# Values of two token tiles by one seven-product multiplication, in a float32 attention kernel with a gate

## The chip, the cores and the metric

The kernel runs on one core of a Trainium2 chip. The metric is the device time of one execution in microseconds (us). TensorE (PE) does matrix products, VectorE (DVE), ScalarE (ACT) and GpSimd (POOL) do elementwise work, and SyncE (SP) issues most transfers. PEld is TensorE's loading of the stationary operand.

## The reference

The input x has 8 batches of 1024 tokens with 512 features, all in float32. With `_layernorm` as usual, the reference is, cut to what matters:

```python
xn = _layernorm(x)
def proj(Wm, bm):                      # 16 heads of 32
    y = einsum('bld,ed->ble', xn, Wm) + bm
    return y.reshape(B, L, H, dk).transpose(0, 2, 1, 3)
q, k, v = proj(Wq, bq), proj(Wk, bk), proj(Wv, bv)
scores = einsum('bhid,bhjd->bhij', q, k) / sqrt(dk)
im = arange(L) % 256
scores = where(im[:, None] >= im[None, :], scores, -1e30)
attn = einsum('bhij,bhjd->bhid', softmax(scores), v)
s = einsum('bld,ed->ble', merge_heads(attn), Wo) + bo
w = (weights >= 0) * 2 - 1
g = silu(clip(einsum('bsi,oi->bso', xn, w) * scale + bias, -100, 100))
out = x + s * g
```

A query sees the keys whose place in their window of 256 is not after its own, in every window. The value product, `xn` with `Wv`, is the one that changes: 1024 x 512 by 512 x 512 in each batch.

## The kernel before

**Tiles.** The 1024 tokens of a batch are dealt to eight token tiles of 128, so that most of the masked part falls on whole tiles that are left out. The normed tokens are turned once into `xnT` (features on partitions). The heads are worked in four groups g of four heads, and each (batch b, group g) has nine steps, n = 0 to 8: 36 steps a batch, 288 in all.

**A step.** Three PSUM uses exist. One tile of four banks, `quad`, holds the scores of a step. It is used twice: first as t, the scores of keys by queries less the row maxima (`probs_quad`, L591 the maxima by matmul, L613 the products), from which ACT takes the exponential p (L626); then as s, scores of queries by keys for the *next* group (`maxima_quad`, L524), from which DVE takes the maxima pm (L536, one reduction or two). So t, exponential, s, reduction, next t form a ring through one PSUM tile. Two banks hold `av`, the sums of p times v (`attend_quad`, L639, a step behind t). The last two banks, `bank(...)`, go in turn to everything else: q, k and v products, gates (y), outputs (o), turned maxima (mT, `shift_rows`, L565, copied out by ACT, L571), turned inputs (xnT) and the sums of p (sum).

`add_probs` (L657) adds the p tiles of a group on POOL, in two running totals, so that the softmax's divisor needs one product with ones (`sum_keys`); for step n it is written in the loop after `attend_quad` of step n, that is a step later than its exponential. ACT copies the sum, DVE inverts it in pieces of 128 columns (`invert`, L714) and multiplies (`normalise_heads`, L718).

**Side work.** TensorE has time in a step between t and s, while ACT works, and between s and the next t, while DVE works. Into these gaps goes side work, in an order written out by hand: `STEADY` for batches 1 to 6, `OPENING` for batch 0, `CLOSING` for batch 7, with one string for each g. V4 is the value product of token tile 4, G2 a gate, q20 the queries of group 2 of the first half of the tokens, O4 an output of the batch before, N0 the layernorm of half of the next batch, W and R turns of Wo and a row of constants, H a gate in plain float32; a prime means the next batch, and what stands before a bar may also be taken early, by the group before. `plan` turns the words into `Work` items, with ACT, DVE, POOL and DMA operations linked some blocks ahead or behind. `Beside.fill` takes items until a wanted time (by the planner's own cost per item) is spent: at least about 1.2 us between t and s, and 2.35 or more between s and the next t. An item whose operands are not written yet is waited for in program order, not skipped, except turns.

`product` makes an item list of one 128 x 512 result: four chunks (one for each 128 features), each of four matmuls that use 32 columns of the array side by side with 512 columns streaming. A chunk can be split at column 192, 256 or 320 to fit what is left of a gap. After the fourth chunk `after` empties the bank: for values one ACT copy (L383). `gate_work` splits the operand in two parts of fewer bits (L427, L428) and makes two passes; DVE and POOL close it (L432, L433, L434), and ACT and DVE finish it later (L438, L441). `output_work` fetches the gate and x again (L728, L730), closes on DVE (L736, L737) and POOL (L738) and stores (L739).

**Start and end.** Before the loop the kernel loads and turns the weights and does the first norms and the first products. After it come the last outputs: `last_output` handles the last tile in two halves of 256 columns (L753, L754 on POOL ahead, L763 the products, L771 and L772 on DVE).

Each engine runs its own instructions in program order; a framework places the semaphores and gives out buffers, so an operation waits for the last reader of the buffer that it writes.

Of the kernel before, what the change touches and what calls it, by code (L numbers as in the profile page):

```python
# [16 lines left out]
P = 128  # L17
# [56 lines left out]
def tile_gated_window_attention(  # L74
# [27 lines left out]
    qk = pool("qk", 3)  # L102
    heads = pool("heads", 6)
    probs = pool("probs", 2)
    total = pool("total", 1)
    tmp = pool("tmp", 5)
    parts = pool("parts", 1)
    rows_p = pool("rows", 1)
    small = pool("small", 4)
    spill = pool("spill", 2, space=bass.MemoryType.DRAM)  # L110
    ps_q = pool("ps_q", 1, space=PSUM)
    ps_a = pool("ps_a", 2, space=PSUM)
# [41 lines left out]
    for it in range(4):  # L154
        load_x(0, it, (nc.sync, nc.scalar)[it % 2])
    fetch_weight("wk", wk, chunks(probs, "p", "wk_st"), [nc.sync, nc.scalar])
    bias_r = temp("bias_r")[0 : 3 * NC, 0:P]
# [10 lines left out]
    for name, src in (("fscale", fscale), ("fbias", fbias), ("bo", bo)):  # L168
# [4 lines left out]
        "wo", wo,  # L173
        [heads.tile([P, 1, D], F32, tag="a0", name=f"wo_st_{o}") for o in range(NC)], [nc.sync],
    )
# [65 lines left out]
    def turn_weight(name):  # L241


        def turn(c):
            if c == 0:
                wT[name] = const.tile(
                    [P, NC, D], F32R if name == "fw" else F32, name=f"{name}T"
                )
            dst = wT[name]
# [11 lines left out]
            if name == "fw":  # L261

                sg = temp(f"sign_{c}")
                nc.vector.tensor_scalar(sg, ps, 0.0, 2.0, ALU.is_ge, ALU.mult)
                nc.vector.tensor_scalar(dst[:, c, :], sg, -1.0, None, ALU.add)
            elif name == "wo":

                nc.scalar.mul(dst[:, c, :], ps, 0.5)
                turned.add(("wo", c))
            elif name == "wk":  # L270
                staged["copy", c] = lambda: (
                    nc.vector.tensor_copy(dst[:, c, :], ps) if c > 1
                    else nc.scalar.copy(dst[:, c, :], ps)
                )
            else:
                evacuate(dst[:, c, :], ps)

        return [lambda c=c: turn(c) for c in range(NC)]


# [97 lines left out]

    def values_work(b, it):
        def after(ps):  # L380

            vt[b, it] = vpool.tile([P, D], F32, tag="v", name=f"v_{b}_{it}")
            nc.scalar.copy(vt[b, it], ps)  # L383

        return product(
            f"v_ps_{b}_{it}",
            [(lambda c=c: (xn_cols(b, it)[:, c, :], wT["wv"][:, c, :])) for c in range(NC)],
            0.86,
            after,
            lambda: (b, it) in turned,  # L390
        )

    def heads_work(b, g, half, which):
# [20 lines left out]
        )  # L414

    def gate_work(b, it, plain=False):

# [4 lines left out]

        def split():
            src = xn_cols(b, it)
            for i in range(2):
                part[i] = parts.tile([P, NC, P], F32R, tag=f"x{i}", name=f"x{i}_{b}_{it}", bufs=2)
            nc.scalar.copy(part[0], src)  # L427
            nc.gpsimd.tensor_tensor(part[1], src, part[0].bitcast(F32), ALU.subtract)  # L428
# [21 lines left out]
        def passes(i):  # L450

            if i == 0:
                hold.append(bank(f"y_ps_{b}_{it}"))
            for c in range(NC):
                nc.tensor.matmul(  # L455
                    hold[0], lhsT=part[i][:, c, :], rhs=wT["fw"][:, c, :],
                    start=(i == 0 and c == 0), stop=(i == 1 and c == NC - 1),
                )
            if i:
                after(hold[0])  # L460

# [22 lines left out]
        )  # L484
        split = Work(0, split, ready=lambda: (b, it) in turned)
        return split, [main], squash, finish
# [160 lines left out]

    def add_probs(b, g, n):

# [11 lines left out]
        for f, j, lo, w, at in segments(n)[0]:  # L661
            if n > TOTAL[f]:
                add(f, n, lo, w, at)
        for f in (0, 1):

            if n == TOTAL[f]:
                for early in range(FIRST[f], n):
# [4 lines left out]
    def keep_sum(b, g, f, ps):  # L672

        aT[b, g, f] = heads.tile([P, HALF], F32, tag=f"a{f}", name=f"aT_{b}_{g}_{f}")
        nc.scalar.copy(aT[b, g, f], ps)  # L675
# [49 lines left out]
    def output_work(b, it):  # L725
        def fetch():
            g = xres.tile([P, D], F32, tag="io", name=f"gb_{b}_{it}")
            nc.sync.dma_start(g, gd[b][it])  # L728
            xr = xres.tile([P, D], F32, tag="io", name=f"xb_{b}_{it}")
            nc.sync.dma_start(xr, tokens(x, b, it))  # L730
# [13 lines left out]
        ]  # L744
        return fetch, product(f"o_ps_{b}_{it}", pairs, 0.86, after, lambda: it in back, True)

# [30 lines left out]
    def row_work():  # L777
# [7 lines left out]
        def after(ps):  # L785
            nc.vector.scalar_tensor_tensor(rows["bo"], rows["bo"], 0.5, ps, ALU.mult, ALU.add)

        return spread, product(
            "bo_ps", [(lambda c=c: (wide[0][:, c, :], wT["wo"][:, c, :])) for c in range(NC)], 0.86, after,
            lambda: bool(wide) and all(("wo", c) in turned for c in range(NC)), True,  # L790
        )

# [8 lines left out]
    STEADY = (  # L801
        "V4 G2 V5 q20 | V7 G3 V6 k20 q21 G4 k21",
        "O4 G5 O5 | q30 N0 k30 O6 q31 G6 k31 G7",
        "N1 O7 O0 | O1 k00' V0' q00' O2 O3 q01'",
        "k01' V1' | q11' G0' V2' k10' G1' V3' k11' q10'",
    )
    OPENING = (
        "V2 G0 V3 V4 G1 V5 V7 V6 G2 k20 q21 k21",
        "G3 q20 q30 N0 k30 | G4 q31 G5 k31 G6 V0'",
        "G7 N1 V1' | k00' q00' W0 V2' W1 V3' W2 q01' W3",  # L810
        "k01' G0' | q11' k10' R G1' k11' q10'",
    )
    CLOSING = (
        "V4 V5 | q20 V7 V6 k20 q21 k21",
        "O4 O5 | q30 k30 O6 q31 O7 k31",
# [17 lines left out]

    blocks, links = [], []

    def link(i, fn, tail=False):
        links.append((i, fn, tail))

    def plan(b, g, text):
        for word in text.split():  # L840
# [26 lines left out]
            elif kind == "V":  # L867
                main = values_work(bb, int(number))
            elif kind == "W":
# [7 lines left out]
            else:  # L877
                split, main, squash, finish = gate_work(bb, int(number), kind == "H")
                if split is not None:
                    link(i - 3, split)  # L880
                later = 1 if b in (0, B - 1) else 0
                link(i + 2 + later, squash)
# [30 lines left out]
    class Beside:  # L913
# [36 lines left out]
        def fill(self, want, kept=None, early=False, turns=1):  # L950
# [5 lines left out]
            while self.work:  # L956
# [15 lines left out]
                elif free and kept is not None:  # L972
                    kept.append(w)
                elif free or spent + w.cost <= want + 0.1:
                    if w.edge:
# [14 lines left out]
                if w.opens:  # L990
                    next_open = since < 9
                since += w.cost
                if w.closes:
# [16 lines left out]
    behind = []  # L1010

    sides = {}

# [15 lines left out]

    idle_turns(44)  # L1030
    for fn in turn_weight("wk"):
        fn()
    stats, scale, normalise, turn = norms[0]
    for k in range(4):
        stats[k]()
        if k % 2:
            scale(k - 1, k + 1)
    for k in range(4):
        normalise[k]()
    staged["copy", 0]()  # L1040
    for k in range(4):
        turn[k]()
        idle_turns(4)
        if k == 1:
            staged["copy", 1]()
    staged["copy", 2]()
    staged["copy", 3]()
    ps = ps_a.tile([P, 512], F32, tag="av", name="bias_ps")
    nc.tensor.transpose(ps[:, 0 : 3 * NC], bias_r, ident[0 : 3 * NC, 0 : 3 * NC])
    nc.scalar.copy(bias_c, ps[:, 0 : 3 * NC])  # L1050
    for w in heads_work(0, 0, 0, "k"):
        w.run()
    more_constants()
# [19 lines left out]

    wv_turns, fw_turns = turn_weight("wv"), turn_weight("fw")
    start = heads_work(0, 0, 1, "k")
    start += woven(heads_work(0, 1, 1, "q"), wv_turns[:2])
    start += woven(heads_work(0, 1, 0, "k"), wv_turns[2:])
    start += values_work(0, 0)
    start += woven(heads_work(0, 1, 1, "k"), fw_turns[:2])
    start += woven(heads_work(0, 1, 0, "q"), fw_turns[2:])  # L1080
    start += values_work(0, 1)
    start = Beside(start, [0] * NQ)
# [12 lines left out]
    for s, (b, g, n) in enumerate(steps):  # L1095
# [12 lines left out]
        def fill(want, kept=None, turns=1):  # L1108

            spent = 0.0  # L1110
            for one in line:
                if spent < want - 0.1:
                    spent += one.fill(want - spent, kept, one is not now, turns)
                if one.work:
                    break
# [3 lines left out]
        if s:  # L1119
# [3 lines left out]
            else:  # L1123
                add_probs(*steps[s - 1])
        if add:
# [7 lines left out]
        if first:  # L1133
            shift_rows(*turn)
        want = max(1.2 - mine, 0.0) if nxt else share
        spent = fill(want, kept, 0)
        if nxt and spent < want - 0.5:
            spent += fill(want - spent, kept)
        share -= spent
        if turn and not first:  # L1140
            shift_rows(*turn)
        if nxt is not None:
# [3 lines left out]
            if n == 8:  # L1146
                shift_parts(0)
        if add:
            invert(*add, 1)
# [15 lines left out]
        spent = now.fill(1e9) if n == NQ - 1 else 0.0  # L1165
        if nxt:
            want = max(share, 2.45 if len(S_QUADS[n]) > 1 else 2.35) - spent
            turned_now = now.turn_ahead()
            want -= turned_now
            want -= fill(want, turns=0 if turned_now else 1)  # L1170
            if want > 0.5:

                want -= fill(want, turns=2)
        if n == NQ - 1:

# [14 lines left out]
    order = (4, 5, 6, 7, 0, 1, 2, 3)  # L1190
    units[4][0]()
    for i, it in enumerate(order):
        if i + 1 < NT:
            units[order[i + 1]][0]()
        if i + 1 < NT and order[i + 1] < 4:
# [56 lines left out]
```

## Time and profile before

| what | value |
|---|---|
| time, median of 3 runs | 2229.66 us (2228.48 to 2230.08) |
| the profiled execution: own time, span | 2227.41 us, 2225.6 us |
| granted TensorE clock in it | 0.999 of full speed |
| busy: PE, POOL, DVE, ACT | 98%, 60%, 57%, 39% |
| first t (L591) of the steps | 77.3 us after the start of the span |
| batches 0 to 6, first t to first t of the next | 272.7, 265.7, 268.5, then 269.25 each (mean of four) |
| last matmul ends, last DVE operation ends | 2216.7, 2222.2 us |
| moved by DMA | 93.60 MB, mean 42 GB/s |
| value products v_ps, L357 | 254.7 us of TensorE matmul busy time, 64 results |

Times inside the kernel come from that one execution. "Busy" is the time that an engine's instructions ran; "idle before, releaser" is the time that the engine stood still before an instruction, and what ended it. A matmul in float32 is recorded as two. The chain that ended last is followed back from the last instruction.

### The profile page before, as it was taken

To read this page: it belongs to the slowest core of one execution; us is meant where nothing else is said; L and a number is where in the kernel's file an instruction comes from. 1 tells how busy PE (TensorE), PEld (TensorE's weight loads), DVE (VectorE), ACT (ScalarE), POOL (GpSimd) and SP (SyncE) were. 2 spreads that over 40 slices of the span, in tenths; PEclk is the share of its full clock that TensorE was granted. 3 is DMA by queue.
4 is the path that set the end of the run, shared out by engine and by line. 5 is a ranking of instruction groups with operands and counts; after the bars stand their busy time and mean duration, and the time that the engine had idled before them with its cause. 6 is when DMAs were issued, how large, how long until landed. Compare 5 with 4: busy or idle time off the path is not lost.

```text
span 2225.6 us, 57271 instructions
## 1 busy us (share of the span) xinstructions
PE 2185.2 (98%) x25989; PEld 858.4 (39%) x25989; DVE 1275.8 (57%) x1635; ACT 875.3 (39%) x862; POOL 1325.8 (60%) x1198
## 2 busy tenths in 40 slices
PE   8999999999999999999999999999999999999998
PEld 4334333343333343333333333344333343333333
DVE  4556556665456655566455655565655665555664
ACT  2244434344334443344434444334434344333331
POOL 1356565666566666576556675557666566665562
PEclk9999999999999999999999999999999999999999
DMA  4001000120001200012000120001100111000113
GB/s 166 3 14 35 11 6 33 50 82 25 25 25 39 81 27 25 25 63 68 16 25 25 63 68 16 25 32 62 62 16 30 40 63 62 7 21 25 44 53 124
DMA packets 49676, 93.60 MB, mean 42 GB/s; under 512 B 5388, under 2 KB 5656, under 8 KB 49432
## 3 DMA queue, kind: packets, MB, share of 16 engines
q1 hardware_dynamic: 48728, 88.76, 12.0%
q8 instruction: 203, 3.33, 0.6%
q10 hardware_dynamic: 704, 1.18, 0.2%
q14 instruction: 41, 0.34, 0.0%
HBM read 56.37 MB, written 33.55 MB: 40 GB/s over the span
## 4 chain that ended last, share of the span: by engine, by line
PE 80%; POOL 6%; DVE 5%; ACT 5%; issue 3%; DMA 1%; SPq 0%; POOLq 0%; ACTq 0%; DVEq 0%
PE s L524 11%; PE av L639 10%; PE t L613 10%; PE v_ps L357 9%; PE q_ps L357 9%; PE k_ps L357 9%; PE o_ps L357 8%; POOL p L657 5%; PE y_ps L455 5%; PE t L591 4%; ACT p L626 4%; DVE pm L536 3%; PE sum L680 2%; PE s L512 1%; PE xnT_ps L327 1%
## 5 line engine op out<-in xcount | busy, mean ns | idle before, releaser
L657 POOL TENSOR_TENSOR p<-p,p 128x512 f32<-128x512 f32 x930 | 1097.7, 1212 | 186.7 <-PE av L639 103.7
L536 DVE TENSOR_REDUCE pm<-s 128x4 f32<-128x2048 f32 (+3 forms) x384 | 663.9, 1750 | 599.0 <-PE s L524 596.8
L626 ACT ACTIVATE p<-t 128x2048 f32<-128x2048 f32 x288 | 541.0, 1878 | 855.8 <-PE t L613 799.9
L714 DVE RECIPROCAL aT<-aT 128x128 f32<-128x128 f32 x256 | 230.3, 928 | 217.8 <-ACT aT L675 217.8
L524 PE MATMUL s<-k,q 32*128 32x512 f32 (+3 forms) x3072 | 315.4, 504 | 7.3 <-ACT p L626 6.5
L639 PE MATMUL av<-p,v 128*32 128x512 f32 (+3 forms) x3072 | 307.4, 495 | 1.6 <-DVE aT L718 1.4
L613 PE MATMUL t<-q,k 32*128 32x512 f32 (+3 forms) x3072 | 306.1, 492 | 0.0
L357 PE MATMUL q_ps<-xnT,wqT 128*32 128x512 f32 (+2 forms) x2656 | 254.5, 497 | 2.0 <-ACT xnT L328 1.0
L357 PE MATMUL k_ps<-xnT,wkT 128*32 128x512 f32 (+2 forms) x2792 | 254.5, 481 | 0.3 <-ACT q L400 0.2
L357 PE MATMUL v_ps<-wvT,xnT 128*32 128x512 f32 (+3 forms) x2720 | 254.7, 490 | 0.0
L357 PE MATMUL o_ps<-woT,aT 128*32 128x512 f32 (+2 forms) x2584 | 243.9, 501 | 1.5 <-ACT shift L571 0.8
L738 POOL TENSOR_TENSOR s<-s,xb 128x512 f32<-128x512 f32 x63 | 86.0, 1365 | 240.6 <-DVE s L737 234.4
L434 POOL TENSOR_SCALAR y<-y 128x512 f32<-128x512 f32 x64 | 39.7, 620 | 276.8 <-DVE y L433 266.4
L428 POOL TENSOR_TENSOR x<-xnT,x 128x512 fp32r<-128x512 f32 x58 | 74.0, 1276 | 165.5 <-ACT x L427 163.1
L613 PEld LDWEIGHTS t<-q,k 32*128 32x128 f32 x3072 | 139.1, 185 | 25.8
L357 PEld LDWEIGHTS k_ps<-xnT,wkT 128*32 128x32 f32 x2792 | 82.5, 109 | 167.6 <-issue 140.5
L357 PEld LDWEIGHTS q_ps<-xnT,wqT 128*32 128x32 f32 x2656 | 78.7, 109 | 174.6 <-issue 151.8
L639 PEld LDWEIGHTS av<-p,v 128*32 128x32 f32 x3072 | 70.3, 108 | 195.9 <-issue 163.4
L357 PEld LDWEIGHTS v_ps<-wvT,xnT 128*32 128x32 f32 x2720 | 78.9, 109 | 168.2 <-issue 143.5
L524 PEld LDWEIGHTS s<-k,q 32*128 32x128 f32 x3072 | 117.0, 184 | 59.9 <-ACT p L626 50.0
L455 PE MATMUL y_ps<-fwT,x 128*128 128x512 f32 x464 | 135.4, 418 | 1.7 <-ACT k L400 1.3
L357 PEld LDWEIGHTS o_ps<-woT,aT 128*32 128x32 f32 x2584 | 76.6, 109 | 152.3 <-issue 134.0
(96 smaller groups left out, 1479.8 us busy)
## 6 DMA issues: line engine op xcount, KB each, us to landing
g<-t SPq DMA_DIRECT2D x64, 256.0 KB, 2.1
gb<-g SPq DMA_DIRECT2D x64, 256.0 KB, 2.9
xb<-in_L_attn_x_dram SPq DMA_DIRECT2D x64, 256.0 KB, 3.3
out_dram<-s SPq DMA_DIRECT2D x63, 256.0 KB, 2.5
x<-in_L_attn_x_dram SPq DMA_DIRECT2D x62, 256.0 KB, 3.1
wq_st<-in_L_attn_Wq_dram SPq DMA_DIRECT2D x2, 512.0 KB, 4.8
wv_st<-in_L_attn_Wv_dram SPq DMA_DIRECT2D x2, 512.0 KB
fw_st<-in_L_ffn_weights_dram SPq DMA_DIRECT2D x2, 512.0 KB, 8.8
```

The source lines that it names most:

```text
L357: nc.tensor.matmul(hold[0][cols, lo:hi], lhsT=lhsT[:, cols], rhs=rhs[:, lo:hi], start=(i == 0 and lo == 0), stop=(i == n - 1), skip_group_ ...
L428: nc.gpsimd.tensor_tensor(part[1], src, part[0].bitcast(F32), ALU.subtract)
L455: nc.tensor.matmul(hold[0], lhsT=part[i][:, c, :], rhs=wT["fw"][:, c, :], start=(i == 0 and c == 0), stop=(i == 1 and c == NC - 1),)
L524: nc.tensor.matmul(sc[:, h, at : at + w], lhsT=qt[b, g][head_rows(h), i * P : (i + 1) * P], rhs=kt[b, g][head_rows(h), lo:hi], start=(at = ...
L536: nc.vector.tensor_reduce(pm[:, 0 if lo == 0 else 1, i, :], sc[:, :, at : at + w], AX.X, ALU.max)
L591: nc.tensor.matmul(sc[:, h, at : at + w], lhsT=neg1[r, :], rhs=shift[b, g, f][r, lo : lo + w], start=(k == 0), stop=False, skip_group_chec ...
L613: nc.tensor.matmul(sc[:, h, at : at + w], lhsT=kt[b, g][head_rows(h), j * P : (j + 1) * P], rhs=qt[b, g][head_rows(h), q0 : q0 + w], start ...
L626: nc.scalar.activation(pt[:, :, :width], sc[:, :, :width], AF.Exp, scale=SCALE)
L639: nc.tensor.matmul(av[b, g, f][head_rows(h), lo : lo + w], lhsT=vt[b, j][:, g * P + h * DK : g * P + (h + 1) * DK], rhs=pts[b, g, n][:, h, ...
L657: nc.gpsimd.tensor_tensor(t[:, hs, lo : lo + w], t[:, hs, lo : lo + w], p[:, hs, at : at + w], ALU.add)
L714: nc.vector.reciprocal(r, r)
L738: nc.gpsimd.tensor_tensor(s, s, xr, ALU.add)
```

## The change

**Values in pairs.** Two value products of token tiles i and j are one product of a 256 x 512 by a 512 x 512 matrix. It is cut into 2 x 2 blocks: the features in halves (X1., X2.), the two token tiles (X.1, X.2), the output columns in halves of 256. Winograd's form of Strassen's multiplication makes the four result blocks from seven block products instead of eight. The four sums S1 to S4 of weight blocks are made once (`sum_blocks`, DVE); the four sums T1 to T4 of token blocks are made by POOL for each pair (`prepare`), while the pair before is at work. The class `Pair` has 14 atoms of four matmuls with 256 columns in four phases, each phase in one bank; two products share a bank's halves, the seventh has a bank alone. `close` empties the phases: 0 by two ACT copies and a POOL add, 1 by three DVE adds, 2 by two ACT copies and two POOL adds, 3 by one DVE add. POOL's adds in a gap before s are put after the reduction is issued (`later`, `defer`). Atoms are not split.

**Around it.** The seven blocks need 14 KB a partition. They share one SBUF tile with Wo: both weights are kept in DRAM (`keep_weight`) and loaded back (`load_weight`) by the words Lo and Lv. The orders are rewritten, with other work between the pairs: words V45, V67 and V01', V23' stand for pairs. The adds of p that go into a total that exists already are written a step earlier, after their own step's s; those that need the total of the step stay (`held`). The parts of a gate have one buffer instead of two, with an order kept. `fill` doesn't open another bank when two are closed behind each other beside a reduction (`shut`), and the loop runs a last closing atom ahead of s if it is ready. The heads pool shrinks from 6 buffers to 5 for one tag.

**Start and end.** wk is requested ahead of the x tiles 2 and 3, and the first keys are made in two halves of 256 tokens. The last outputs fetch two tiles ahead instead of one, with x in another pool, in batch 7.

The order of instructions gives 1792 value matmuls of 256 columns, where there were 688 of 512, 312 of 320 and of 192 columns and 48 of 256. DVE gets 132 adds of 128 x 256 more, ACT 128 copies of 256 columns for 64 of 512, POOL 224 operations of 128 x 256 more.

```diff
@@ product of a pair
-    def values_work(b, it):
-        def after(ps):
-            vt[b, it] = vpool.tile([P, D], F32, tag="v", name=f"v_{b}_{it}")
-            nc.scalar.copy(vt[b, it], ps)
...
+    def sum_blocks():
+        for out, a, b, op in (
+            ("S1", "A21", "A22", ALU.add),
+            ("S3", "A11", "A21", ALU.subtract),
+            ("S2", "S1", "A11", ALU.subtract),
+            ("S4", "A12", "S2", ALU.subtract),
+        ):
+            nc.vector.tensor_tensor(wb[out], wb[a], wb[b], op)
+
+    def keep_weight(name):
+        weight_d[name] = kept_w.tile(list(wb["tile"].shape), F32, tag=name, name=f"{name}_d")
+        nc.sync.dma_start(weight_d[name], wb["tile"])
+        wb["name"] = name
+
+    def load_weight(name):
+        shared_tile(name)
+        nc.sync.dma_start(wb["tile"], weight_d[name])
+        wb["name"] = name
...
+    class Pair:
...
+            phases = (
+                (("X11", "A11"), ("T2", "S2")),
+                (("T3", "S3"), ("T1", "S1")),
+                (("T4", "A22"), ("X22", "S4")),
+                (("X21", "A12"),),
+            )
+
+            def matmul(k, part, c):
+                if part == 0 and c == 0:
+                    hold.append(bank(f"{name}_ps_{k}"))
+                lhs, rhs = phases[k][part]
+                for q in range(NH):
+                    cols = head_rows(q)
+                    nc.tensor.matmul(
+                        hold[k][cols, part * 256 : part * 256 + 256],
+                        lhsT=self.t[lhs][:, c, cols], rhs=wb[rhs][:, c, :],
...
+                if part + 1 == len(phases[k]) and c == 1:
+                    close(k, hold[k])
...
+        def prepare(self):
...
+            for out, a, b in (
+                ("T1", "X12", "X11"), ("T2", "X22", "T1"), ("T3", "X22", "X12"), ("T4", "X21", "T2"),
+            ):
+                nc.gpsimd.tensor_tensor(t[out], t[a], t[b], ALU.subtract)
+            self.prepared = True
...
+        def close(k, ps):
+
+            if k == 0:
+                u[0], u[1] = part_sum(name, 0), part_sum(name, 1)
+                nc.scalar.copy(u[0], ps[:, LO])
+                nc.scalar.copy(u[1], ps[:, HI])
+                later(lambda: plus(u[1], u[1], u[0], nc.gpsimd))
+            elif k == 1:
...
+                plus(u[2], ps[:, LO], u[1])
+                plus(vt[b, j][:, HI], ps[:, HI], u[2])
+                plus(u[3], ps[:, HI], u[1])
+            elif k == 2:
+                y21, y12 = vt[b, i][:, HI], vt[b, j][:, LO]
+                nc.scalar.copy(y21, ps[:, LO])
+                nc.scalar.copy(y12, ps[:, HI])
+                later(lambda: plus(y21, y21, u[2], nc.gpsimd))
+                later(lambda: plus(y12, y12, u[3], nc.gpsimd))
+            else:
+                plus(vt[b, i][:, LO], ps[:, LO], u[0])
@@ adds of p
         for f, j, lo, w, at in segments(n)[0]:
-            if n > TOTAL[f]:
+            if n > TOTAL[f] and not held:
                 add(f, n, lo, w, at)
         for f in (0, 1):
-
-            if n == TOTAL[f]:
+            if n == TOTAL[f] and held:
...
@@ orders
     STEADY = (
-        "V4 G2 V5 q20 | V7 G3 V6 k20 q21 G4 k21",
-        "O4 G5 O5 | q30 N0 k30 O6 q31 G6 k31 G7",
-        "N1 O7 O0 | O1 k00' V0' q00' O2 O3 q01'",
-        "k01' V1' | q11' G0' V2' k10' G1' V3' k11' q10'",
+        "V45 G2 | q20 V67 Lo G3 k20 q21 G4 k21",
+        "O4 O5 G5 O6 O7 | q30 N0 k30 q31 G6 k31 N1 G7",
+        "O0 O1 O2 O3 Lv | k00' q00' k01' q01'",
+        "V01' G0' | q11' V23' k10' G1' k11' q10'",
     )
     OPENING = (
-        "V2 G0 V3 V4 G1 V5 V7 V6 G2 k20 q21 k21",
-        "G3 q20 q30 N0 k30 | G4 q31 G5 k31 G6 V0'",
-        "G7 N1 V1' | k00' q00' W0 V2' W1 V3' W2 q01' W3",
-        "k01' G0' | q11' k10' R G1' k11' q10'",
+        "V23 G0 V45 | G1 V67 k20 G2 q21 k21",
+        "G3 W0 q20 W1 G4 | q30 W2 N0 k30 W3 G5 R q31 Lv N1 G6 k31",
+        "G7 V01' | k00' q00' k01' q01'",
+        "G0' V23' | q11' k10' G1' k11' q10'",
     )
     CLOSING = (
-        "V4 V5 | q20 V7 V6 k20 q21 k21",
+        "V45 | q20 V67 Lo k20 q21 k21",
...
-                later = 1 if b in (0, B - 1) else 0
+                later = 1 if b == 0 else 0
@@ step loop
             else:
-                add_probs(*steps[s - 1])
+                add_probs(*steps[s - 1], held=True)
...
+        defer[0] = kept
         spent = fill(want, kept, 0)
...
+        if nxt:
+
+            ahead = next((w for w in now.work if w.cost), None)
+            if ahead and ahead.closes and ahead.slow and ahead.cost < 0.5 and ahead.ready():
+                spent += fill(ahead.cost, kept, 0)
+        defer[0] = None
...
+        if not last:
+
+            add_probs(b, g, n)
         if add:
             invert(*add, 1)
@@ tail
-    units[4][0]()
+    for it in order[:2]:
+        units[it][0]()
     for i, it in enumerate(order):
-        if i + 1 < NT:
-            units[order[i + 1]][0]()
+        if i + 2 < NT:
+            units[order[i + 2]][0]()
```

## The prediction

> **What bounds the kernel now.** The page comes first: the share of each engine, then the chain that ended last, then the costliest groups.
>
> ```profile
> span 2225.6 us, 57271 instructions
> ...
> PE 2185.2 (98%) x25989; PEld 858.4 (39%) x25989; DVE 1275.8 (57%) x1635; ACT 875.3 (39%) x862; POOL 1325.8 (60%) x1198
> ...
> PE 80%; POOL 6%; DVE 5%; ACT 5%; issue 3%; DMA 1%; SPq 0%; POOLq 0%; ACTq 0%; DVEq 0%
> ...
> L657 POOL TENSOR_TENSOR p<-p,p 128x512 f32<-128x512 f32 x930 | 1097.7, 1212 | 186.7 <-PE av L639 103.7
> L536 DVE TENSOR_REDUCE pm<-s 128x4 f32<-128x2048 f32 (+3 forms) x384 | 663.9, 1750 | 599.0 <-PE s L524 596.8
> L626 ACT ACTIVATE p<-t 128x2048 f32<-128x2048 f32 x288 | 541.0, 1878 | 855.8 <-PE t L613 799.9
> ...
> L357 PE MATMUL v_ps<-wvT,xnT 128*32 128x512 f32 (+3 forms) x2720 | 254.7, 490 | 0.0
> ```
>
> TensorE is busy 98% of the span and carries 80% of the chain. So matmul time is worth what it costs, wherever something else does not set the pace. What that something is shows in one step, from one t to the next, in the timeline of batch 3:
>
> ```profile
> 884.12 0.40 PE L591 MATMUL t<-shift,neg 3*128 3x512 bf16 x4
> ...
> 885.52 1.88 ACT L626 ACTIVATE p<-t 128x2048 f32<-128x2048 f32 x1 [1.43 <-PE t L613]
> ...
> 887.05 0.41 PE L565 MATMUL mT_ps<-identb,mt 128*32 128x128 bf16 x16
> ...
> 887.45 1.14 PE L524 MATMUL s<-k,q 32*128 32x512 f32 x8
> 887.50 0.59 ACT L571 CAST shift<-mT_ps 128x512 bf16<-128x512 f32 x1
> ...
> 888.52 1.92 PE L357 MATMUL v_ps<-wvT,xnT 128*32 128x512 f32 x16
> 888.66 2.29 DVE L536 TENSOR_REDUCE pm<-s 128x4 f32<-128x2048 f32 x1 [0.91 <-PE s L524]
> ...
> 891.50 0.40 PE L591 MATMUL t<-shift,neg 3*128 3x512 bf16 x4
> ```
>
> t and s share the one quad. The exponential ends at 887.40 and s starts at 887.45. The reduction ends at 890.95, and only then may the next t start; here it starts 0.55 later, since values and gate matmuls fill TensorE to 891.50. A step has thus a floor: s no earlier than 3.35 after t, the next t no earlier than 3.55 after s, 6.9 in all (up to 7.35 for n = 5, 6, 8, which have a second reduction). Side work up to the floor is free; above it every us counts. The stages by the starts of t in the trace: batch 0 from 77.3 to 350, then 265.7, 268.5 and four times 269.25 for batches 1 to 6, then batch 7, whose first 27 steps take 193.3, 7.16 each: at the floor. A steady step takes 7.48, a little over it.
>
> Two waits and the tail matter beside this:
>
> ```profile
> ACT p L626 <- POOL p L657: 55.8, 20, 5.9
> ```
> ```profile
> L763 PE MATMUL o_ps<-woT,aT x64: 376/379/403, 2212.8 to 2216.3; 128*32 128x256 f32 x64
> ```
> ```profile
> 2215.00 0.54 SPq L730 DMA_DIRECT2D xb<-in_L_attn_x_dram  x1
> 2217.34 1.26 POOL L753 TENSOR_TENSOR s<-gb,bo_r 128x512 f32<-128x512 f32 x1 [3.71 <-DMA gb<-g]
> ...
> 2219.98 0.42 DVE L771 TENSOR_TENSOR s<-o_ps,gb 128x256 f32<-128x256 f32 x1 [5.41 <-POOL xb L754]
> ...
> 2221.82 0.42 DVE L772 TENSOR_TENSOR s<-s,xb 128x256 f32<-128x256 f32 x1
> ```
>
> The exponential of g = 2, n = 3 is late once in a batch, because the adds of L657 that read its buffer run late; TensorE loses about 1.0 there (most of ACT's wait is slack). At the end the matmuls are done at 2216.7, but the last gate and x were fetched so late that DVE starts 3.3 later.
>
> **Part 1, the values on TensorE.** A chunk of four 512-column matmuls runs in 0.859, start to start, so a pair of token tiles costs 8 x 0.86 = 6.88. The change has 14 atoms of four 256-column matmuls. The L763 row is such work: eight groups (each f32 matmul is recorded twice) in 3.81 with a pause of 0.42, so 0.42 each; I take 0.43, half a chunk, 6.02 a pair. Bounds: 0.476 with the pause, a gain of only 0.2 a pair, and 0.42. So -0.86 a pair and -3.44 a batch.
>
> [...]
>
> **Part 2, what sinks in the floor.** Batch 7: nothing is gained, its steps are at the floor. Batch 0: four of its steps (one near the end of g = 2, three at the end of g = 3) end up with no side work and sit at the floor, and work that batch 0 did ahead for batch 1 no longer runs there; of the 3.44 I count -0.4 there and -1.3 in batch 1. Batches 2 to 6: -3.44 each. Gates move from splits around s (two passes of 1.13) to both together (2.05) in about five of eight tiles: between 0 and -1.0 a batch; taken -0.5.
>
> **Part 3, adds moved a step earlier** (`held`): the wait above goes, -1.0 for each of batches 2 to 6. What is late next are the closes of Part 4.
>
> **Part 4, the closes.** Each pair has four phases over the two side banks. It adds ACT copies of 256 columns (about 0.37, between 0.585 for 512 and 0.169 for 12), DVE adds (0.42, the L771 row) and POOL adds (about 0.72, between 620 for the one-input row and 1008 for 128x384). Totals: DVE 128 x 0.42 = 54, POOL 224 x 0.72 = 161, ACT 128 x 0.37 - 64 x 0.585 = 10. POOL goes from 60% to 67% and DVE to 60%; no engine becomes the bound. The cost is latency, as s stands behind these matmuls in TensorE's order. In a steady batch:
> - g = 0, n = 0 (V45): a k2 atom stands ahead of s and needs the bank of mT. ACT frees that after the exponential (3.30) and the 0.59 copy, near 4.0; the atom adds 0.43 and s starts near 4.6, not 3.35: +1.2.
> - g = 0, n = 4 (V67): k3 needs the bank that DVE frees with three adds, the first of which waits for POOL's u1 behind four adds of L657 (4.95): +0.5.
> - g = 3, n = 0 (V01'): mT needs the bank of k0, freed by two copies behind the exponential, 3.30 + 0.74 + 0.1; mT's 0.34 follows and s starts at 4.5: +1.2. V23' clears its bank by about 0.5: nothing.
>
> Sum +2.9 a batch; ends 0 (the order of ACT hides it) and 5 (V23' and both reductions late too). Batch 0 has V23, V45 and V67 nearly back to back: the same u1 wait at steps 3, 5 and 6 gives 2.3 + 1.75 + 0.55, 0.75 at V01', and the block sums on DVE (4 x 0.7, ahead of a reduction) 1.3 past slack: +6.7 in all. Batch 1: +1.6 (V45 and V67). Batch 7: A as above 1.35, one more reduction 0.4, mT behind a plain gate's close 1.25, less 0.9 of the old wait: +2.1.
>
> [...] With u1 on DVE the waits through POOL would be some 0.42 instead of up to 2.3, which is worth 4 us of this sum.
>
> **Part 5, the shared weight tile.** Lo and Lv are two issues on SP a batch; 1.84 MB at the 166 GB/s of the first slice is 11 us, and two to four steps (15 to 30 us) lie between the last reader and the first user. An issue takes SP 0.6; behind it wait x and gate fetches, which come a step or more ahead. Cost 0; without the cover, up to 11 a load.
>
> **Part 6, start and end.** wk is requested ahead of two x tiles and the first keys start with half the tokens. The first k_ps starts at 16.4 and wkT waits 1.5 for its DMA: -2.4, between -4 and 0. The tail fetches two tiles ahead: the fetched pair lands before the matmuls end, so DVE starts at its last matmul (2216.7 + 0.2), and one 512 add leaves its way: between -3.1 and -5.0; taken -4.5.
>
> **Sum.** Batches 2 to 6: -3.44 - 0.5 - 1.0 + 2.9 = -2.04 each, -10.2; batch 2 starts 0.75 below the others, +0.8. Batch 0: -0.4 + 6.7 = +6.3; batch 1: -1.3 + 1.6 = +0.3; batch 7: +2.1. Start and end -2.4 - 4.5 = -6.9. Total -7.6. The profiled run took 2227.41 (span 2225.6 and 1.8 around it) and lies 2.25 below the median 2229.66. The change moves all alike: 2229.66 - 7.6, about 2222. About 0.2%, 4.5 us, is what a measurement here can tell from no change.
>
> **Rivals.**
> - The full gain: no close delays s. Then 14.5 + 1.6 + 2.1 + 6.7 of delays go: 2222 - 25 = 2197; half of them gone is 2209. For: TensorE's waits so far are 21 us in the whole span, and the two banks already turn over at ACT's speed. Against: each place named has an instruction ahead of s. Chance 0.15.
> - Slower, one mechanism: the k1 close. Its three DVE adds (1.25) wait for POOL, and where they stand ahead of the maximum (L536) the next t is late by the whole close, at every pair. My delays are 25 us over 32 pairs, 0.78 each; at 1.0 the gain is gone; at 1.25 they are 40, and the time is 2222 + 15 = 2237. For: POOL's queue is 5 long at L657, DVE has to end its reduction 3.55 after s. Against: most k1 closes fall after the reduction was issued. Chance 0.27.
> - Delays of about 1.0 a pair, no change: 2229. Chance 0.1.
> - It does not do what it says: an atom costs 0.476, so the values gain 6 instead of 27.5 us: -7.6 + 17 or so, 2239; or Wv comes back late. Chance 0.05.
> - My forecast, 2222 with 2214 to 2227 as its own range: 0.43.
>
> Of these, 0.54 lie more than 4.5 us below, 0.18 within it, 0.28 above. The range, 2205 to 2240, leaves out the lower half of the full gain and the worst of the slow cases.
>
> **What would show it.** v_ps rows with 256 columns, 0.43 apart; steady batches near 267.2; the wait of the exponential on L657 gone; s at 4.5 to 4.6 after t at g = 0 and g = 3, n = 0; batch 0 about 6 longer; the last DVE operation within 2 us of the last matmul. If the DVE row of the k1 close shows long waits on POOL and pm starts late in most pair steps, the second rival is right; if steady batches are at 264 or less, the first is.

## The result and the profile after

The changed kernel takes 2236.24 us (median of 6 runs, 2234.48 to 2236.78), beside 2228.47 (2224.61 to 2230.08) of the kernel before on the same chips: a ratio of 1.0036, 95% interval 1.0023 to 1.0049. It is slower by 8 us, where 7.6 less were forecast. In the profiled executions the span goes from 2225.6 to 2234.5. The page after, sections 1, 2 and 5:

```profile
span 2234.5 us, 60376 instructions
...
PE 2162.9 (97%) x27151; PEld 902.1 (40%) x27151; DVE 1332.1 (60%) x1769; ACT 880.7 (39%) x928; POOL 1487.3 (67%) x1422
...
PEclk9999998999999999999999999999999999999999
...
L477 PE MATMUL v_ps<-wv_shared,v_t 128*32 128x256 f32 x2048 | 127.6, 381 | 5.5 <-ACT shift L739 5.3
```

POOL and DVE grew as worked out (67% and 60%). TensorE is busy 22 us less, yet the span is longer. The new thing is one digit: the granted clock has an 8 in the seventh slice, 335 to 391 us. The first t of each batch, from the trace, gives the account, in us:

| stage | before | after | change | forecast |
|---|---|---|---|---|
| start to the first t | 77.3 | 78.2 | +0.9 | -2.4 |
| batch 0 | 272.7 | 283.0 | +10.3 | +6.3 |
| batch 1 | 265.7 | 266.7 | +1.0 | +0.3 |
| batches 2 to 6 | 1345.4 | 1343.9 | -1.5 | -9.4 |
| batch 7, 27 steps | 193.3 | 196.4 | +3.1 | +2.1 |
| the rest | 71.2 | 66.3 | -4.9 | -4.5 |

**Batch 0: the clock.** A table by stretches of 8 us (busy time by engine, the granted clock as the third value from the end, then DMA):

```profile
236.00:244.00 8.00, 6.22 (x64) 2.08 (x60) 4.10 (x3) 3.74 (x4) 7.61 (x13) 1.00 0.10 36
244.00:252.00 8.00, 8.00 (x70) 2.36 (x72) 1.48 (x1) 5.10 (x7) 7.21 (x7) 0.79 0.00 0
...
348.00:356.00 8.00, 5.59 (x52) 2.34 (x48) 2.29 (x1) 1.94 (x2) 0.14 (x1) 0.64 0.00 0
356.00:364.00 8.00, 5.18 (x44) 1.42 (x40) 5.84 (x12) 0.93 (x2) 7.42 (x7) 0.71 0.00 0
```

The timeline of TensorE in the same kernel, two like groups of av and what stands before the second:

```profile
285.76 1.06 PE L807 MATMUL av<-p,v 128*32 128x512 f32 x8
...
351.20 0.61 PE L759 MATMUL t<-shift,neg 3*128 3x384 bf16 x8 [2.41 <-DVE pm L704]
...
353.78 1.93 PE L807 MATMUL av<-p,v 128*32 128x512 f32 x8
```

After a pause of 2.41 the same eight matmuls take 1.93 instead of 1.06. The trace's clock record has half the clock from 244.4, 292.2, 350.2 and 360.4 us, for 3.41, 3.41, 6.83 and 6.83 us. Each follows a pause of TensorE of 1.8 to 2.8 us, at the steps 20, 26, 34 and 35 of the count (36 to a batch, from 0). (A fifth, of 3.41, falls on the last steps at 2169.5.) The kernel before has no such stretch between its first t and its last outputs. At step 35 it has values and queries of the next batch where TensorE now pauses. Before, and then after:

```profile
347.28 1.06 PE L357 MATMUL v_ps<-wvT,xnT 128*32 128x512 f32 x8
348.16 1.91 PE L357 MATMUL q_ps<-xnT,wqT 128*32 128x512 f32 x24
350.00 0.39 PE L591 MATMUL t<-shift,neg 3*128 3x512 bf16 x4
```
```profile
357.35 1.04 PE L692 MATMUL s<-k,q 32*128 32x128 f32 x16
361.20 0.61 PE L759 MATMUL t<-shift,neg 3*128 3x512 bf16 x4 [2.81 <-DVE pm L704]
```

**Steady batches.** TensorE's waits in batch 4, before:

```profile
PE s L524 <- ACT p L626: 0.9, 1, 0.9
```

and after:

```profile
PE t L759 <- DVE pm L704: 1.5, 2, 1.1
PE v_ps L477 <- ACT shift L739: 0.9, 1, 0.9
PE mT_ps L733 <- ACT v_u L533: 0.7, 1, 0.7
PE k_ps L423 <- ACT xnT L394: 0.7, 1, 0.7
PE mT_ps L733 <- DVE y L597: 0.4, 1, 0.4
PE v_ps L477 <- DVE v_u L455: 0.4, 1, 0.4
```

Before, two rows of 0.2 stand beside the one shown: 1.3 in all, now 4.6. Rows two, three and six are the three closes of the forecast. Row one was not foreseen: at g = 2, n = 2 an output, not a pair, is closed ahead of the reduction.

```profile
1319.07 0.67 DVE L908 TENSOR_TENSOR o_ps<-o_ps,bo_r 128x512 f32<-128x512 f32 x1
...
1319.78 0.69 DVE L909 TENSOR_TENSOR s<-o_ps,gb 128x512 f32<-128x512 f32 x1
...
1320.39 2.28 DVE L704 TENSOR_REDUCE pm<-s 128x4 f32<-128x2048 f32 x1
...
1322.72 0.40 PE L759 MATMUL t<-shift,neg 3*128 3x512 bf16 x4 [1.09 <-DVE pm L704]
```

s was issued at 1317.77; a reciprocal and the two adds keep DVE to 1320.4, and t comes at 1322.72.

**The end** is as forecast: the operands of the last output are there before its matmuls are done. DVE's last operation starts 0.55 after the end of the last matmul (2230.17 against 2229.62), where it started 5.1 after it (2221.82 against 2216.7).

```profile
2225.64 1.28 POOL L926 TENSOR_TENSOR s<-gb,bo_r 128x512 f32<-128x512 f32 x1 [0.17 <-DMA gb<-g]
2225.81 3.81 PE L936 MATMUL o_ps<-wo_shared,aT 128*32 128x256 f32 x64
...
2228.32 0.42 DVE L944 TENSOR_TENSOR s<-o_ps,gb 128x256 f32<-128x256 f32 x1 [0.77 <-POOL xb L927]
...
2230.17 0.43 DVE L945 TENSOR_TENSOR s<-s,xb 128x256 f32<-128x256 f32 x1
```

The wait for that DMA was 3.71 and is 0.17; DVE's wait for POOL was 5.41 and is 0.77.

### The profile page after: what moved, and what is told of

The parts are those of the page before. It is cut to its first block, busy times and chain, and to the rows that moved or that the text cites. A ratio compares the mean times of both kernels' runs of the same rounds, so it can differ in the third digit from the quotient of the medians.

```text
span 2234.5 us, 60376 instructions
## 1 busy us (share of the span) xinstructions
PE 2162.9 (97%) x27151; PEld 902.1 (40%) x27151; DVE 1332.1 (60%) x1769; ACT 880.7 (39%) x928; POOL 1487.3 (67%) x1422
## 5 line engine op out<-in xcount | busy, mean ns | idle before, releaser
L884 DVE RECIPROCAL aT<-aT 128x128 f32<-128x128 f32 x256 | 230.9, 929 | 209.6 <-ACT aT L845 209.5
L423 PE MATMUL k_ps<-xnT,wkT 128*32 128x512 f32 (+3 forms) x2800 | 255.2, 481 | 6.4 <-ACT xnT L394 5.0
L423 PE MATMUL q_ps<-xnT,wqT 128*32 128x512 f32 (+3 forms) x2824 | 256.2, 479 | 0.9 <-ACT xnT L394 0.7
L423 PE MATMUL o_ps<-wo_shared,aT 128*32 128x512 f32 (+2 forms) x2688 | 242.5, 488 | 0.2 <-DVE y L597 0.2
L423 PEld LDWEIGHTS q_ps<-xnT,wqT 128*32 128x32 f32 x2824 | 84.0, 110 | 167.9 <-issue 138.3
L423 PEld LDWEIGHTS o_ps<-wo_shared,aT 128*32 128x32 f32 x2688 | 81.0, 110 | 174.3 <-issue 146.6
L759 PE MATMUL t<-shift,neg 3*128 3x512 bf16 (+3 forms) x1536 | 114.7, 330 | 25.1 <-DVE pm L704 21.3
L477 PE MATMUL v_ps<-wv_shared,v_t 128*32 128x256 f32 x2048 | 127.6, 381 | 5.5 <-ACT shift L739 5.3
L619 PE MATMUL y_ps<-fwT,x 128*128 128x512 f32 x464 | 127.5, 410 | 1.9 <-ACT shift L739 0.8
```

Source lines behind the costliest of these rows:

```text
L423: nc.tensor.matmul(hold[0][cols, lo:hi], lhsT=lhsT[:, cols], rhs=rhs[:, lo:hi], start=(i == 0 and lo == 0), stop=(i == n - 1), skip_group_ ...
L477: nc.tensor.matmul(hold[k][cols, part * 256 : part * 256 + 256], lhsT=self.t[lhs][:, c, cols], rhs=wb[rhs][:, c, :], start=(part == 0 and ...
L619: nc.tensor.matmul(hold[0], lhsT=part[i][:, c, :], rhs=wT["fw"][:, c, :], start=(i == 0 and c == 0), stop=(i == 1 and c == NC - 1),)
L759: nc.tensor.matmul(sc[:, h, at : at + w], lhsT=neg1[r, :], rhs=shift[b, g, f][r, lo : lo + w], start=(k == 0), stop=False, skip_group_chec ...
L884: nc.vector.reciprocal(r, r)
```

## The experiments

Ratios are to the kernel before on the same chip, from 5 to 11 executions of each kernel (one in experiment 2), with 95% intervals. Stages and steps come from one profiled execution each.

**1. TensorE kept busy in the pauses (warm).** At steps 20, 26, 34 and 35 of the count, into a side bank:

```diff
+    def busy_turns(n):
+        if n:
+            spare = bank(f"spare_{step_now[0]}")
+            for _ in range(n):
+                nc.tensor.transpose(spare[:, 0:P], ident, ident)
...
+    at_turn, at_end = {20: 12}, {26: 12, 34: 15, 35: 15}
```

> The changed kernel with 54 unneeded 128 x 128 transposes of the identity on TensorE in four steps of batch 0 (steps 20, 26, 34 and 35 of the count), where its trace shows TensorE paused 1.8 to 2.8 us and then every matmul at twice its time for some 3.4 us. Theory (the clock): the four slow stretches cost 1.8 + 1.2 + 2.7 + 2.9 = 8.6 us; with TensorE kept busy the granted clock is 0.999 instead of 0.995 and the time 2236.2 - 8.6 = 2227.6, within 2. Rival (the closes of the pairs hold the reduction, step by step): the pauses are what costs, the transposes only fill them, and the time stays at 2235 to 2238.

Measured: 2229.3 us, ratio 1.0008 (0.9999 to 1.0017), against 1.0036: 0.28%, 6 us, come back by adding work. The same stretches of its trace:

```profile
244.00:252.00 8.00, 7.56 (x82) 2.82 (x82) 2.10 (x1) 5.71 (x8) 7.60 (x7) 1.00 0.01 2
...
348.00:356.00 8.00, 6.62 (x87) 3.88 (x85) 3.97 (x4) 2.36 (x2) 4.42 (x5) 1.00 0.01 2
356.00:364.00 8.00, 7.80 (x96) 2.90 (x96) 6.69 (x13) 2.98 (x3) 4.47 (x4) 1.00 0.00 0
```

All at full clock. Steps 21, 27, 35 and 36 went from 9.06, 8.46, 10.00 and 9.75 to 7.61, 6.88, 7.19 and 6.88: 8.7 us. Of these 8.7 the two executions differ by 6.0 in all: the new one starts 0.8 later, and its stage after batch 7's 27 steps is 2.0 longer, with half clock for 6.83 instead of 3.41. (It has half clock for 3.41 at step 3 too, which steps 4 and 5 win back.) The theory holds, the rival falls.

**2. What a pause does by itself (pauses).** On the kernel before:

```diff
+    longer = {
+        (b, g, n): b + 1 for b in range(1, 7) for g, n in ((2, 3), (3, 6), (0, 4))
+    }
...
+        for _ in range(longer.get((b, g, n), 0)):
+            nc.vector.tensor_reduce(spare_m, sc[:, :, 0:128], AX.X, ALU.max)
```

> The kernel before with extra reductions of 512 columns (0.67 each) between s and its own reduction in three steps of each of batches 1 to 6, two extra in batch 1 and one more in each further batch, so that TensorE pauses some 0.8 to 4.2 us there. Theory (a pause by itself slows the clock): after pauses of about 1.8 and more the matmuls of the next steps run at twice their time for some 3.4 us, after pauses under 1.5 they don't; the granted clock falls to about 0.99. Rival (the clock falls where TensorE has too little work over many steps, as at batch 0's end): no slow stretch after any of the 18 pauses, clock 0.999. The outputs are the same; only time is added.

Measured (one execution): 2313.0 us, clock 0.982. Three of the 18 pauses in TensorE's timeline, each with the first av after it:

```profile
720.58 0.40 PE L598 MATMUL t<-shift,neg 3*128 3x512 bf16 x4 [1.75 <-DVE pm L543]
...
721.88 1.06 PE L646 MATMUL av<-p,v 128*32 128x512 f32 x8
```
```profile
592.13 0.40 PE L598 MATMUL t<-shift,neg 3*128 3x384 bf16 x8 [1.81 <-DVE pm L543]
...
593.88 1.93 PE L646 MATMUL av<-p,v 128*32 128x512 f32 x8
```
```profile
1440.72 0.61 PE L598 MATMUL t<-shift,neg 3*128 3x384 bf16 x8 [3.93 <-DVE pm L543]
...
1443.29 1.94 PE L646 MATMUL av<-p,v 128*32 128x512 f32 x8
```

Of the made pauses the four of 1.35 to 1.75 left the clock alone. All 14 of 1.81 to 4.72 were followed by half clock: for 3.41 us after the two near 1.8, for 3.41 or 6.83 after those of 2.5 to 3.2, for 6.83 after all from 3.27 on. So a pause does it, in a batch full of work too, and the rival falls.

The length of the pause alone does not decide, however. In experiment 5's trace the same pause of step 35, again of 2.81, left the clock alone:

```profile
358.43 0.40 PE L759 MATMUL t<-shift,neg 3*128 3x512 bf16 x4 [2.81 <-DVE pm L704]
...
359.61 1.07 PE L807 MATMUL av<-p,v 128*32 128x384 f32 x16
```

In the clock record of the changed kernel every change after 244.4 stands at a whole multiple of 3.4133 from there, within 0.02. So I laid windows of that length over its trace, counted from 244.4, and over experiment 5's, counted from its change at 128.4. The two windows about the pause of step 35, first in the changed kernel, then in experiment 5 (the first busy time is that of TensorE's matmuls):

```profile
357.04:360.45 3.41, 1.35 (x24) 0.55 (x20) 2.46 (x3) 0.59 (x1) 3.41 (x5) 1.00 0.00 0
360.45:363.87 3.42, 2.67 (x16) 0.87 (x20) 3.25 (x10) 0.21 (x1) 2.97 (x3) 0.50 0.00 0
```
```profile
353.70:357.11 3.41, 1.91 (x28) 0.55 (x20) 1.90 (x3) 0.58 (x1) 3.41 (x4) 1.00 0.00 0
357.11:360.52 3.41, 2.09 (x32) 0.94 (x35) 3.24 (x10) 0.70 (x1) 3.33 (x4) 1.00 0.00 0
```

In the changed kernel TensorE was idle for 2.06 of one window, and the next has half clock. In experiment 5 a window's end split the pause, 1.50 and 1.32 were idle, and the clock stayed. From 35 us on, in the traces of the changed kernel and of the kernel before (there counted from its only change, at 2219.0), all six windows at full clock with 1.92 to 3.41 idle were followed by half clock, none of the 1267 with 1.50 or less, and of the three between the one with 1.78 but not those with 1.80 and 1.88.

**3. The new orders with plain values (plain_v_warm).** Pairs replaced, Wv and Wo resident:

```diff
-                pair = values_pair(bb, *(int(n) for n in number))
-                pairs[-1].then_prepare(pair)
-                pairs.append(pair)
-                blocks.append(Block((b, g), pair.halves[0]))
-                main = pair.halves[1]
+                blocks.append(Block((b, g), values_work(bb, int(number[0]))))
+                main = values_work(bb, int(number[1]))
```

> The changed kernel with its values by the plain product of the kernel before (two for each pair, at the same places), Wv and Wo in tiles of their own without reloads, and 23 unneeded transposes where batch 0 has no side work (steps 34 and 35). All else as changed. Theory (the clock took the gain, the pairs themselves break about even): 3.4 us of TensorE more in each steady batch, 2.5 of waits less, batch 0 about 6 less: 2225, and 2 or 3 below the kernel with pairs and transposes. Rival (closes cost 1.25 a pair, 40 in all, against 27 of gain): 2227.6 - 13 = 2215.

Measured: 2222.69, ratio 0.9981 (0.9972 to 0.9989); 6.6 us under the kernel with pairs and transposes on the same chip, between the two expectations. By stages (against warm): batch 0 271.2 against 277.1, a steady batch 269.4 against 268.8, batch 7's 27 steps 193.4 against 196.5. The pairs win 0.6 in a steady batch and lose 6 in batch 0 and 3 in batch 7. Step 35 has no side work in this kernel either (15 transposes stand there): the new orders leave it empty, not the pairs alone.

**4. The tail and the earlier adds alone (before_tail_adds).** On the kernel before, the tail hunk and the `held` hunks of the change, nothing else.

> The kernel before with two of the other changes alone: the last outputs fetch two tiles ahead (x from the other pool), and the adds of p are written a step earlier. Values as before. Theory: the tail gives 4.9 as in the trace of the change, the wait of the exponential for POOL goes at 0.9 in each of batches 1 to 6: 2228.5 - 10.3 = 2218. Rival (the earlier adds only move the wait to another reader of POOL): 2223.5, the tail alone.

Measured: 2215.36 (2213.95 to 2217.02), ratio 0.9944 (0.9931 to 0.9956): 12 us faster than before, the fastest of all. The rest after batch 7's 27 steps is 67.7 instead of 71.2, batches 3 to 6 are 268.1 to 268.3 instead of 269.25, and TensorE's rows of waits in batch 4 come to 0.4. The theory holds, with other sizes by stage: the end gives 3.5 and not 4.9, batch 1 gives 0.9, batch 2 3.0 (TensorE's rows of waits for the exponential fall from 3.1 to 0.5 there), and batches 3 to 6 1.1 each. So the rest of the change costs some 20 us on top of these two parts. By the ratios, about 8 of them come with the new orders and what else goes with them, under plain values (experiment 3), 6 more with the pairs (experiment 1), and 6 with the clock (the change without transposes).

**5. One add from POOL to DVE (u1_dve).**

```diff
-                later(lambda: plus(u[1], u[1], u[0], nc.gpsimd))
+                later(lambda: plus(u[1], u[1], u[0]))
```

> The changed kernel with one edit: the add of phase 0 (u1 = u1 + u0) on DVE instead of POOL. Theory: the waits of the close of phase 1 for POOL go (1.95 and 1.87 at steps 3 and 5 of batch 0, 0.4 a steady batch), 32 DVE adds of 0.42 come, hidden: 2236.2 - 5 = 2231. Rival (POOL's queue holds up the close at every pair): 2220 or less.

Measured: 2237.31 (2234.69 to 2239.82), ratio 1.0046 (1.0032 to 1.0060): no gain. Steps 3 and 5 fell as expected (9.54 to 7.59, 9.34 to 7.47), but step 6 rose from 8.81 to 12.14, with half clock from 128.4, and step g = 0, n = 0 of batches 2 to 7 by 0.86 (in batch 4 from 8.23 to 9.09). There the three adds of the close stand ahead of the reduction on DVE already in the changed kernel; with one add more the reduction starts 6.76 after t instead of 5.90. The wait only changed its engine; the expectation left out that queue, and my estimate of 4 us for this move in the forecast was wrong.

**6. The planner held back (paced).** On the kernel of experiment 1:

```diff
-                elif w.opens and shut["banks"] == 2:
+                elif w.opens and (shut["banks"] == 2 or shut["turn"] and w.cost == 0.43):
                     break
+                elif w.closes and w.slow and shut["sum"]:
+                    break
...
+        shut.update(turn=bool(turn), sum=bool(add))
         spent = fill(want, kept, 0)
```

> The changed kernel with the 54 unneeded transposes, and with the planner changed in two places: in steps with a turn of maxima (n = 0 and 7) no phase of a pair is opened ahead of s, and in steps with a sum of p no output or phase that DVE empties is closed ahead of s. Theory (waits at g = 0, n = 0, at g = 3, n = 0, and an output's close ahead of the reduction at g = 2, n = 2, take the steady gain: 1.1, 0.9 and 1.2 in the trace): these three go, 0.4 each of matmuls move behind s; steady batches 268.8 - 1.8 = 267, the time 2229.3 - 11 = 2218. Rival (steady batches are bound by TensorE's matmuls, waits only take the place of them): 2228 or more.

Measured: 2223.41, ratio 0.9987 (0.9978 to 0.9996), some 5 under experiment 1 by the ratios, less than half of the 11 expected. Steady batches 267.4 instead of 268.8. Step g = 2, n = 2 fell from 8.32 to 7.43. Step g = 0, n = 0 did not fall (8.23 to 8.36), although s starts at 3.32 instead of 4.37: the atoms and the close held back are late behind s. At g = 3 the two steps n = 0 and 1 together fell from 15.06 to 14.6 (14.89 in batch 4). So of the three waits the output's close could be taken away by order, for 0.9; of the two at the pairs one gave 0.45 and the other moved.

**7. The same rule with plain values (plain_paced).**

> The kernel with plain values and the new orders (plain_v_warm), with the planner rule of the kernel paced, so that no output is closed ahead of s in a step with a sum of p. Theory (the new orders lose 1.2 a steady batch to the output's close ahead of the reduction at g = 2, n = 2): that wait goes, 0.3 come back: 2222.7 - 5 = 2217.5, about the kernel before with tail and adds alone (2215). Rival (the orders lose by the amount of matmul work or by the gates): no change, 2222.

Measured: 2219.17, ratio 0.9963 (0.9949 to 0.9977) after 0.9981 without the rule: some 4 us, with steady batches 268.5 instead of 269.4. The new orders themselves had this wait.

**8. Batch 0's own values plain (best).** Plain chunks of 2 x 256 columns from the blocks, pairs from batch 1 on, block sums made later:

```diff
+            elif kind == "V" and bb == 0:
+                blocks.append(Block((b, g), plain_values(0, int(number[0]))))
+                main = plain_values(0, int(number[1]))
```

> The kernel with the changed planner rule (paced), but batch 0's own values by plain products from the same weight blocks; pairs from batch 1 on; the block sums made later, in batch 0's first group. Unneeded transposes stay at four places. Theory (pairs cost batch 0 5.9 by the waits of their closes and the block sums): 5 less than the kernel paced, about 2213. Rival (batch 0 is bound by the amount of matmul work): no gain, or 2 more than paced.

Measured: 2220.23, ratio 0.9972 (0.9961 to 0.9983); beside paced 3 less, but the intervals overlap, and batch 0 is 277.2 against 278.3. Steps 3 and 5 fell by 1.6 and 1.4, step 18, the start of the next pair, rose from 7.45 to 9.39, as the close there waits in its turn. Inconclusive.

**9. The pairs without POOL (no_pool).** T sums and POOL's adds left out:

```diff
-                nc.gpsimd.tensor_tensor(t[out], t[a], t[b], ALU.subtract)
+                t[out] = t[a]
```

> The changed kernel with the 54 unneeded transposes, and all of the pairs' POOL work left out: the four sums T (the products take one of the two operands instead), the add of phase 0 and the two of phase 2. 224 operations of 0.73, 164 us of POOL. The outputs are not the reference's. Theory (POOL's queue costs batch 0, where the closes wait for it at steps 3, 5 and 33 and the layernorm's small operations stand behind it at step 20, and little elsewhere): batch 0 about 6 shorter, a steady batch 0.4, the time 2229.3 - 8.5 = 2221. Rival (POOL's queue delays every pair): steady batches at 267 or less, the time 2212.

Measured: 2218.0, ratio 0.9960 (0.9947 to 0.9972). Batch 0 is 271.5 instead of 277.1, a steady batch 268.0 instead of 268.8. So POOL's 164 us cost 6 in batch 0 and 0.8 in a steady batch; the rival's 267 was not reached. What the queue does is seen in the changed kernel's timeline at step 20 (POOL, then TensorE), one of the pauses that halved the clock:

```profile
239.15 1.42 POOL L455 TENSOR_TENSOR v<-v,v_u 128x256 f32<-128x256 f32 x2
240.63 0.23 POOL L364 TENSOR_SCALAR rstd<-mv 128x4 f32<-128x4 f32 x1
...
243.50 0.66 PE L393 MATMUL xnT_ps<-ident,x 128*128 128x128 f32 x4 [1.78 <-ACT x L381]
```

Four adds of p (from 230.9), four T sums and two closes (236.3 to 240.6) stand ahead of the layernorm's small operation; ACT's normalising waited for it until 242.6, and TensorE's turns until 243.5. Without the pairs' POOL work it follows the adds of p at once, and the turns wait for nothing:

```profile
232.75 0.23 POOL L371 TENSOR_SCALAR rstd<-mv 128x4 f32<-128x4 f32 x1
...
237.97 1.53 PE L354 MATMUL spare<-ident 128*128 128x128 f32 x12
239.65 0.63 PE L401 MATMUL xnT_ps<-ident,x 128*128 128x128 f32 x4
```

Step 20 itself is only 0.2 shorter (9.07 for 9.27), as the 12 transposes stand there still.

## Why the prediction was wrong

**Right.** Part 1: half a chunk was a good price; v_ps matmuls of 256 columns show 381 ns as the L763 row did, and in a steady batch 3.3 more waits and 0.5 less time leave 3.8 less of matmuls (3.44 + 0.5 forecast). Part 3: the row s <- p of 0.9 is gone. Part 4's prices: POOL 0.73 (0.72), DVE 0.42, and of the three places 0.9, 0.4 and 0.7 were seen for 1.2, 0.5 and 1.2. Part 5: no row shows TensorE waiting for a weight. Part 6, the tail: -4.9 (-4.5), though the same tail gave only 3.5 in experiment 4.

**The step that failed** is Part 2, "what sinks in the floor". It counted steps without side work as idle, a saving lost and nothing more. A pause of TensorE was not free here: the four pauses left 1.78 to 2.20 us of a window of 3.413 idle, and after each the matmuls ran at half clock for 3.41 or 6.83. That cost 7.3 us after three such steps (26, 34 and 35) and 1.45 after step 20, whose pause has another cause (below). The kernel before has work in those steps; the new orders, and seven products for eight, took it away. Experiments 1 and 2 show the clock's part.

**A second step** is Part 3 with the orders: "what is late next" was sought among the pairs' closes alone. The rewritten order put an output's close ahead of a reduction that a reciprocal already held up, 1.1 in every steady batch (experiments 6 and 7), and xnT and gate closes add 1.1 in rows four and five. Waits rose by 3.3, not 1.9, and steady batches gave 0.3 each on average, not 2. POOL's queue was followed to the closes but not to the layernorm that it was moved ahead of (step 20, experiment 9).

**Luck.** Without the clock's 8.7 us, batch 0 would stand at +4.4 and batch 1 at -1.8, each some 2 under its forecast (+6.3 and +0.3). The other terms there were too dear by some 4 in all and hid half of what the clock cost.

**The start** gave +0.9 where -2.4 was forecast. The first t stands at 77.1, 77.3 and 78.9 in the three traces with the old start and at 77.8 to 79.1 in the eight with the new one: the gain did not come, and no run tells why.

**The rivals.** The slower one named 2237 and the time came there, but not by its mechanism: DVE's k1 closes do wait for POOL (30.1 us over 16 times in the trace), while TensorE waits for them 0.4 a steady batch and 4.3 in batch 0. The adds of the close stand ahead of the reduction at g = 0, n = 0, but that step, with the late s, is 0.85 longer once a batch, not 1.25 at every pair. Most of the loss was clock and orders. The full gain is refuted by the sign that it named: steady batches came at 268.8, not at 264 or less, and at 267.4 with closes held back (experiment 6).

**Batch 7** lost 3.1 (+2.1 forecast), about where it was looked for: 2.6 in its first five steps (the first from 6.88 to 8.35) and 1.4 at g = 1, n = 7 (6.95 to 8.37, mT behind a gate's close, for 1.25 forecast), less 0.9 elsewhere.

**What stays open:** what the rewritten orders lose beside the output's close (with experiment 7's rule and plain values the time is still some 4 us over experiment 4).

## What to carry to other kernels

When a change takes matmuls away, look where TensorE will stand still, and for how long: in a step whose pace another engine sets, a pause can cost time in the steps after it (here 8.7 us after four pauses), and needless matmuls there can pay (here 6 us). Follow each new operation on a shared in-order queue to everything that it now stands ahead of, small operations of other stages too. And run the parts of a bundled change apart: here two small parts gave 12 us, and the rest took back 20.

## What the runs showed of the hardware

In the changed kernel's trace TensorE's clock changed at 244.4 us and after that only at whole multiples of 3.4133 from there, within 0.02. In that trace and the one of the kernel before, from 35 us on, half clock followed each of the six windows at full clock in which TensorE's matmuls left 1.92 us or more idle, none of the 1267 with 1.50 or less, and one of three between. The place of a pause counted beside its length: at step 35 one of 2.81 was followed by half clock in the changed kernel, with 2.06 idle in one window, and not in experiment 5, with 1.50 and 1.32 in two. Pauses of 1.78 (step 20) and 1.88 (step 3) differ too: the first was followed by half clock, the second was not.

In the changed kernel half clock went on after the two slow windows with 0.99 and 0.75 idle, which makes the two of 6.83, and ended after the five with none.

Unneeded transposes kept the clock up as well: with them, in experiment 1, it is 1.00 in the stretches 244 to 252, 348 to 356 and 356 to 364, where the changed kernel has 0.79, 0.64 and 0.71.
